# The fifth chunk of k of two attention layers, from one seven-product scheme instead of plain products in each layer

## The chip, the cores and the metric

The kernel runs on one core of one Trainium2 chip. The metric is the device time of one execution, in microseconds (us). All times here are of this one core. TensorE multiplies matrices and is called PE in the profile; VectorE is DVE, ScalarE is ACT, GpSimdE is POOL and SyncE is SP, which only issues loads and stores here. PEld is TensorE's loading of weights, which runs beside its products.

## The reference

Two cross-attention layers follow each other. Each takes the same 722 context tokens per sample (8 samples); the last 77 of them are text, the first 645 are "ip" tokens. There are 100 queries per sample, 640 channels, 20 heads of 32 channels, and context channels are 1024. Cut to what matters, one layer is:

```python
q      = x @ Wq                         # 8 x 100 x 640
k_text = text @ Wk;    v_text = text @ Wv
k_ip   = ip @ Wk_ip;   v_ip   = ip @ Wv_ip          # 8 x 645 x 640, the large products
out_text = softmax(q k_text^T * scale) v_text       # by head
sem      = q_sem . ip * scale                       # second layer only: a score per query and ip token
out_ip   = softmax(q k_ip^T * scale + 0.5 * sem) * mask @ v_ip
x = (out_text + out_ip) @ Wo + bo + x
```

The first layer has no `sem` and no mask. `k_ip` and `v_ip` depend on the context and on the layer's weights alone, not on x, so both layers' can be made at any time before they are used. Everything is float32.

## The kernel before, in words

**Units, pairs, blocks, chunks.** A unit u is a sample in a layer: u = 8 * layer + sample, 16 units in all. Two units that follow each other are a pair (8 pairs: `PAIRS`, units 0 and 1 to units 14 and 15; `LAST` is the eighth). The 645 ip tokens are five blocks (`BLOCKS`: four of 128 and one of 133). The 640 outputs of k, in rows, are five chunks of 128; chunks 0 to 3 are made together, chunk 4 is the "fifth chunk".

**Making k and v.** For each pair and block, k and v are made from the context (`x_all`, three places for a block of both samples, loaded by `load_x` in two transfers) and the weights W["k", ...] and W["v", ...]. Both use `seven` (L179): the product of a 2 by 2 block matrix of tokens (two samples by two halves of the 1024 channels) with a 2 by 2 block matrix of weights (two halves of the channels by two halves of the outputs) is made with seven products of quarters instead of eight. It costs sums: of weights, once per layer (`weight_sums`, L133 to L136), and of tokens, for each block (`token_sums`, L231: on DVE s1 at L232 and s2 at L233; s4 later by `fourth_sum`, L527 in the profile). The seven steps come in the order first, sixth, second, seventh, fifth, fourth, third. Step names mark their PSUM tile: psv_a (first and second share it), psv_b (sixth), psv_c, psv_d, psv_e. Each step's result goes from PSUM to an SBUF tile at once: first and second on ACT (L193, L202), the others on DVE (L198, L208, L213, L219, L224). The first step needs only loaded tokens; the sixth needs s2. PSUM's pool for products has two banks.

v of a block is seven steps of four matmuls (L597), with 320 columns, or 397 where the first layer's text is carried along. Chunks 0 to 3 of k are seven steps of L625: for a group of two blocks, one set for each half of the chunks; for the fifth block alone, both halves together, with 133 columns.

**The fifth chunk of k.** It has no second half of outputs to be paired with. `last_k` (L563) makes it with plain products: 8 matmuls over the 8 eighths of the channels, two samples side by side in the columns (256, or 266 in the fifth block), in two halves of four matmuls. A matmul shows as two records in the trace. The result is copied by ACT (L570) and written to `k_d` by POOL (two transfers, L572). Its weights are `W["k", 4]`, a tile loaded by `load_wk4` (one transfer of 512 KB per layer). `head` puts, ahead of the steps for v of a block, `begin` (the sums s1 and s2) and the two halves of `last_k`.

**Attention.** There are 80 steps: a unit and a chunk (four heads) each. A step makes scores against the first 512 tokens (L952, part 0), transposes of the step before (L1043, `pspt`), the scores against the other 210 (part 1), further transposes, and the products with v of the step before (`values`, L1065), copied to `hs` by DVE (L1069). The softmax of scores goes over DVE (maxima: L961 in the first layer, L967 in the second, where sem is added) and ACT (exponentials L975). Factors (DVE, L997 to L1001), scaling (ACT, four L1007; DVE L1011, L1015) follow. These pieces are put into a list, `later`, and written out one at a time: a task of production that costs time emits one piece (`next_task`); `scores` part 0 and the first transposes emit all that are left.

**Order of the work.** The order on PE, DVE and ACT is that of the program (`manual_schedule`); SP and POOL are ordered by the scheduler. k and v of pair 0 are made ahead of attention. The production of pair g + 1 is a list of tasks with costs (1.8 for a k step, 2.15 or 2.67 for v, 0 for loads and sums) that `spread` lays between the steps of the pair before, by a plan of intervals (`production`); `between` and `make` put them in. `insert` places weight loads and sums of weights at marks in the lists ("fifth j", "v j", "k j"). So layer 0's pairs 1 to 3 are made in steps 0 to 28.8, layer 1's pairs 4 to 6 in steps 28.8 to 58.8, the last pair in steps 58.8 to 78.95. The last pair is made otherwise: `last_visits` brings blocks in again, `two_chunks` (10 visits, L736 to L741) makes two chunks of k and of v at once, and `fifth_chunk` (L767) makes the fifth of k and of v by plain products (L780, L786), in 8 visits: k and v together for two blocks, then k for three, then v for three. The plan has the boundaries n + 2.9, n + 6.9 and n + 8.95, where n is step 70.

The fifth chunk is used last in a unit, as its fifth attention step (in the last pair too).

Of the kernel before, what the change touches and what calls it, by code (L numbers as in the profile page):

```python
# [28 lines left out]
NCC = CC // P  # L29
# [5 lines left out]
HK = NCC // 2  # L35
NB = 5
BLOCKS = [(j * P, (j + 1) * P if j < NB - 1 else NI) for j in range(NB)]
# [7 lines left out]
def two_layer_xattn(  # L45
# [101 lines left out]
    def load_wk(src):  # L147
        load_quarters("k", src, 2 * P)
        load_wk4(src)
# [26 lines left out]
    def product_ps(name):  # L176
        return pj[0].tile([P, 512], F32, tag="pj", name=name)
# [64 lines left out]
    with ExitStack() as es:  # L242
# [172 lines left out]
        with tc.manual_schedule(engines={mybir.EngineType.PE}):  # L415
            sums_of("k")
            text_sums()
            text_k(0)
            load_wk(wkt[1])
            text_v(0)  # L420
            sums_of("v")
            load_left(0)
            text_v_blocks(0)
            load_wv(wvt[1])
            sums_of("k")
            text_k(1)
            load_wk(wki[0])
            left_v(0)
            load_left(1)
            left_text()  # L430
            text_v(1)
            sums_of("v")
            for f in weight_sums("k", 2 * P):
                f()
            text_v_blocks(1)
            left_v(1)
# [68 lines left out]

    def quarters(at, n):
        return [x_all[:, at, i, HK * h : HK * (h + 1), :n] for i in range(2) for h in range(2)]

# [2 lines left out]
    def pair_tasks(us):  # L513
# [15 lines left out]
        for js in ((0, 1), (2, 3), (4,)):  # L529
# [15 lines left out]
            def operands(which, j, js=js, n=n, st=st, pos=pos):  # L545
# [8 lines left out]
                    return lambda k: x_all[:, at[j], i, HK * h + k, :n]  # L554
                lo, hi = sorted(at[j] for j in js)
                return lambda k: x_all[:, lo : hi + 1 : hi - lo, i, HK * h + k, :n]

            def last_k(j, half, n=n, open_={}):
                if half == 0:
                    open_[j] = product_ps(f"psk4_{us[0]}_{j}")  # L560
                ps = open_[j]
                for k in range(HK * half, HK * (half + 1)):
                    nc.tensor.matmul(  # L563
                        ps[:, : 2 * n], lhsT=W["k", 4][:, k, :], rhs=x_all[:, at[j], :, k, :n],
                        start=(k == 0), stop=(k == NCC - 1),
                    )
                if half == 0:
                    return
                o = opool.tile([P, 2, NX], F32, tag="k4", name=f"k4_{us[0]}_{j}")
                nc.scalar.copy(o[:, :, :n], ps[:, : 2 * n].rearrange("p (i n) -> p i n", i=2))  # L570
                for h, u in enumerate(us):
                    nc.gpsimd.dma_start(k_d[u][:, 4, BLOCKS[j][0] : BLOCKS[j][1]], o[:, h, :n])  # L572

            def v_steps(j, operands=operands):
                made, vo, gst = {}, {}, {}
# [188 lines left out]
        sums_ = [(0.0, lambda i=i: late[i]()) for i in range(2)]  # L764
        return begin, steps[:1] + sums_[:1] + steps[1:4] + sums_[1:] + steps[4:]

    def fifth_chunk(kinds, j, xs, at):  # L767
        n0, n1 = BLOCKS[j]
        tasks = []
        for kind in kinds:  # L770
            n = n1 - n0 if kind == "k" else P
            open_ = {}

            def half(h, kind=kind, n=n, open_=open_):
                if h == 0:
                    open_[0] = product_ps(f"ps{kind}5_{j}")
                ps = open_[0]
                if kind == "k":
                    for k in range(HK * h, HK * (h + 1)):
                        nc.tensor.matmul(  # L780
                            ps[:, : 2 * n], lhsT=W["k", 4][:, k, :], rhs=x_all[:, xs[at], :, k, :n],
                            start=(k == 0), stop=(k == NCC - 1),
                        )
                else:
                    for k in range(NCC):
                        nc.tensor.matmul(  # L786
                            ps[:, h * P : (h + 1) * P], lhsT=x_all[:, xs[at], h, k, :P],
                            rhs=wide[("wv00", "wv10")[k // HK]][:, k % HK, 2 * P : 3 * P],
                            start=(h == 0 and k == 0), stop=(k == NCC - 1), skip_group_check=True,
                        )  # L790
                if h == 0:
                    return
                t = opool.tile([P, 2, NX], F32, tag="k4", name=f"o5_{kind}_{j}")
                nc.scalar.copy(t[:, :, :n], ps[:, : 2 * n].rearrange("p (i n) -> p i n", i=2))
                for i, u in enumerate(LAST):
                    if kind == "k":
                        nc.gpsimd.dma_start(k_d[u][:, 4, n0:n1], t[:, i, :n])
                    else:
                        nc.gpsimd.dma_start(v_d[u][j * P : (j + 1) * P, 4 * P :], t[:, i, :P])

            tasks += [(1.8, lambda h=h, f=half: f(h)) for h in range(2)]
        return None, tasks


    sem_state, gs = {}, {}
# [268 lines left out]
    def production():  # L1074

        plan = []
        all_tasks = [pair_tasks(PAIRS[i]) for i in range(1, len(PAIRS) - 1)]
        parts = {}

        def sums_later(kind, n, i):  # L1080
            if kind not in parts:
                parts[kind] = weight_sums(kind, n)
            parts[kind][i]()
            if i == 3:
                del parts[kind]
# [265 lines left out]
```

## Time and profile before

| | before |
|---|---|
| median of 3 runs | 2067.76 us (2067.09 to 2068.76) |
| the profiled execution's own time | 2067.52 us |
| its span | 2065.8 us |
| granted TensorE clock, mean | 0.998 |
| DMA moved | 255.38 MB, 124 GB/s |
| stretch 0 to 225 us: TensorE, DVE, ACT busy | 219.31, 47.23, 22.29 us |
| 392 to 1050 (pairs 1 to 3 are made) | 657.33, 364.33, 267.72 of 658 |
| 1300 to 1733 (the rest of pairs 4 to 6) | 431.42, 250.82, 192.84 of 433 |
| 1733 to 1965 (the last pair, first part) | 227.18, 178.15, 132.27 of 232 |
| 1965 to 2034 (its end, steps 73 to 78) | 66.50, 53.57, 52.28 of 69 |
| 2034 to 2066 (the last step) | 24.99, 14.86, 12.51 of 32 |

The profiled execution takes 1.7 us more than its span, which runs from the first to the last instruction that the profile shows. The attention starts at about 392 us (the first maxima are at 392.2). A busy TensorE is not a stopped TensorE, but matmuls are pipelined, so a record's duration is longer than the distance to the next one's start, and prices are best read from starts in the timeline.

### The profile page before, as it was taken

To read this page: it belongs to the slowest core of one execution; us is meant where nothing else is said; L and a number is where in the kernel's file an instruction comes from. 1 tells how busy PE (TensorE), PEld (TensorE's weight loads), DVE (VectorE), ACT (ScalarE), POOL (GpSimd) and SP (SyncE) were. 2 spreads that over 40 slices of the span, in tenths; PEclk is the share of its full clock that TensorE was granted. 3 is DMA by queue.
4 is the path that set the end of the run, shared out by engine and by line. 5 is a ranking of instruction groups with operands and counts; after the bars stand their busy time and mean duration, and the time that the engine had idled before them with its cause. 6 is when DMAs were issued, how large, how long until landed. Compare 5 with 4: busy or idle time off the path is not lost.

```text
span 2065.8 us, 38497 instructions
## 1 busy us (share of the span) xinstructions
PE 2043.4 (99%) x15122; PEld 1579.3 (76%) x15122; DVE 1096.4 (53%) x2989; ACT 793.5 (38%) x2271; POOL 309.1 (15%) x445
## 2 busy tenths in 40 slices
PE   9999999999999999999999999999999999999998
PEld 8676767677778777786778777787878778888776
DVE  2211222356555655555575655556565657787775
ACT  1001000144433434334343443345444445555575
POOL 3212312111111111010110110010112011111110
PEclk9999999999999999999999999999999999999999
DMA  9545313332424443262544442262435255554471
GB/s 335 150 134 169 96 56 105 88 107 71 129 83 131 130 111 93 81 174 70 158 142 123 135 113 83 84 178 75 115 86 148 82 143 139 160 137 131 138 210 52
DMA packets 302547, 255.38 MB, mean 124 GB/s; under 512 B 46686, under 2 KB 271378, under 8 KB 302366
## 3 DMA queue, kind: packets, MB, share of 16 engines
q1 hardware_dynamic: 280590, 184.48, 32.9%
q0 software_dynamic: 21776, 68.44, 9.8%
q8 instruction: 119, 1.95, 0.4%
q14 instruction: 62, 0.51, 0.1%
HBM read 183.93 MB, written 68.93 MB: 122 GB/s over the span
## 4 chain that ended last, share of the span: by engine, by line
PE 97%; DVE 2%; ACT 1%; issue 0%; DMA 0%; SPq 0%; DVEq 0%; ACTq 0%
PE psv_a L597 8%; PE psv_d L597 8%; PE pspt L1043 8%; PE psk_a L625 6%; PE psk L563 6%; PE psk_d L625 6%; PE sc L952 6%; PE pv L1065 5%; PE psv_e L597 4%; PE psv_c L597 4%; PE psv_b L597 4%; PE psk_e L625 3%; PE psk_b L625 3%; PE psk_c L625 3%; PE pso L863 3%; PE psq L275 2%
## 5 line engine op out<-in xcount | busy, mean ns | idle before, releaser
L1050 DVE COPY pt<-pspt 128x400 f32<-128x400 f32 (+1 forms) x319 | 175.2, 569 | 147.6 <-PE pspt L1043 146.3
L975 ACT ACTIVATE p<-sc,st 100x512 f32<-100x512 f32 (+1 forms) x320 | 166.0, 531 | 198.9 <-DVE st L961 125.4
L1007 ACT ACTIVATE p<-p,st 100x512 f32<-100x512 f32 x320 | 207.5, 713 | 58.6 <-DVE st L1001 58.4
L1043 PEld LDWEIGHTS pspt<-ident,p 100*128 100x128 f32 (+1 forms) x1920 | 189.4, 138 | 46.4 <-ACT p L1007 5.6
L1043 PE MATMUL pspt<-ident,p 100*128 100x100 f32 (+1 forms) x1920 | 213.6, 251 | 8.6 <-ACT p L1007 3.0
L975 ACT ACTIVATE p<-p,st 100x512 f32<-100x512 f32 (+1 forms) x320 | 176.8, 554 | 99.0 <-DVE st L967 99.0
L597 PE MATMUL psv_a<-wv,x 128*128 128x397 f32 (+1 forms) x560 | 184.9, 472 | 0.0
L646 POOL DMA_DIRECT2D k_d<-ko x140 | 99.8, 717 | 525.5 <-DVE ko L219 477.4
L1048 ACT COPY pt<-pspt 128x400 f32<-128x400 f32 x161 | 79.3, 493 | 252.1 <-PE pspt L1043 251.9
L597 PE MATMUL psv_d<-wv,s 128*128 128x320 f32 (+1 forms) x560 | 174.9, 455 | 0.0
L597 PEld LDWEIGHTS psv_a<-wv,x 128*128 128x128 f32 x560 | 103.6, 189 | 62.1 <-issue 8.1
L967 DVE CUSTOM_DVE_ANT_0 p<-sc,sem 100x512 f32<-100x512 f32 (+1 forms) x320 | 138.8, 490 | 21.2 <-PE sc L952 20.5
L597 PEld LDWEIGHTS psv_d<-wv,s 128*128 128x128 f32 x560 | 103.4, 190 | 57.5 <-issue 5.5
L961 DVE TENSOR_REDUCE st<-sc 100x2 f32<-100x1024 f32 (+1 forms) x160 | 125.2, 824 | 30.3 <-PE sc L952 30.3
L952 PE MATMUL sc<-k,q 32*100 32x210 f32 (+1 forms) x1280 | 138.5, 502 | 0.0
L625 PE MATMUL psk_d<-s,wk 128*128 128x256 f32 (+1 forms) x672 | 136.4, 348 | 0.0
L625 PE MATMUL psk_a<-x,wk 128*128 128x256 f32 (+1 forms) x672 | 135.5, 346 | 0.0
L612 POOL DMA_DIRECT2D v_d<-vo x70 | 38.5, 550 | 634.0 <-DVE gst L587 311.1
L563 PE MATMUL psk<-x,wk 128*128 128x256 f32 (+1 forms) x560 | 132.1, 383 | 0.0
L625 PEld LDWEIGHTS psk_a<-x,wk 128*128 128x128 f32 x672 | 109.2, 189 | 20.4 <-issue 6.0
L563 PEld LDWEIGHTS psk<-x,wk 128*128 128x128 f32 x560 | 102.5, 188 | 26.1 <-issue 9.9
L625 PEld LDWEIGHTS psk_d<-s,wk 128*128 128x128 f32 x672 | 108.1, 189 | 17.8 <-issue 5.2
(209 smaller groups left out, 3252.5 us busy)
## 6 DMA issues: line engine op xcount, KB each, us to landing
x<-ip_t SPq DMA_DIRECT2D x84, 512.0 KB
k<-k_d SPq DMA_DIRECT2D x80, 322.5 KB
v<-v_d SPq DMA_DIRECT2D x80, 320.0 KB
v_d<-vo POOLq DMA_DIRECT2D x70, 320.0 KB, 2.5
k_d<-ko POOLq DMA_DIRECT2D x112, 128.0 KB, 4.8
x<-ip_t SPq DMA_DIRECT2D x22, 532.0 KB
o<-wo SPq DMA_DIRECT2D x35, 320.0 KB
q<-wq SPq DMA_DIRECT2D x20, 320.0 KB
```

Source lines behind the costliest of these rows:

```text
L563: nc.tensor.matmul(ps[:, : 2 * n], lhsT=W["k", 4][:, k, :], rhs=x_all[:, at[j], :, k, :n], start=(k == 0), stop=(k == NCC - 1),)
L597: nc.tensor.matmul(ps[:, :m], lhsT=tokens(k)[:, :P], rhs=w[:, k, :], start=(k == 0 and not go_on), stop=(k == HK - 1), skip_group_check=True,)
L625: nc.tensor.matmul(ps[:, i * m : (i + 1) * m], lhsT=W["k", WHICH[which]][:, k, r * P : (r + 1) * P], rhs=tokens(k), start=(i == 0 and k == ...
L646: nc.gpsimd.dma_start(dst[:, :, r], ko[0][:, h, :, i, p0 : p0 + n])
L952: nc.tensor.matmul(scs[i // 2][:S, i % 2, : k1 - k0], lhsT=qs_[u][rows, c, :], rhs=ks[u, c][rows, k0:k1], start=True, stop=True)
L961: nc.vector.tensor_reduce(st[:, part, 2 * h : 2 * h + 2], scs[h][:S, :, :n], AX.X, ALU.max, negate=True)
L967: nc.vector.tensor_tensor_reduce(out=p[:, i, k0 : k0 + n], in0=scs[h][:S, i % 2, :n], in1=sems[u][:, k0 : k0 + n], scale=-1.0, scalar=3.0e ...
L975: nc.scalar.activation(dst, dst if l else scs[h][:S, i % 2, :n], AF.Exp, bias=st[:, part, i : i + 1], scale=-1.0 if l else 1.0, accum_out= ...
L1007: nc.scalar.activation(p[:, i, :KA], p[:, i, :KA], AF.Copy, scale=mul[:, 0, i : i + 1])
L1043: nc.tensor.transpose(ps[:rows, i * S : (i + 1) * S], pr[u, c][:, i, j * P : j * P + rows], ident[:S, :S])
L1050: nc.vector.tensor_copy(dst, src)
L1065: nc.tensor.matmul(ps[32 * i : 32 * i + 32, :S], lhsT=lhs, rhs=pt[:rows, j, i * S : (i + 1) * S], start=(j == 0), stop=(j == 5),)
```

## The change

The fifth chunks of both layers are paired with each other. The token matrix is as before; the weight matrix has the two halves of the channels by the two layers. One scheme of seven products, `k4_steps`, thus makes the fifth chunk of k for both layers, in the pairs of the first layer, and writes it to `k_d` of units u and u + 8. For a group of two blocks a step is four matmuls with 256 columns, and 133 for the fifth block alone (four transfers to `k_d` per block). It uses the sums s1, s2 and s4 that `begin` made for the group. The pairs of the second layer make no fifth chunk of k.

The weights of this scheme, b11 to b22 and the sums t2 to t4 (t1 is written over b12), are 256 KB tiles (`W4`): two in the place of the old `wk4` tile, two in the two buffers "sem", and three in "g", "kt5" and "gt", tiles that the second layer's semantic scores use. `load_w4` issues four transfers; `w4_sums` makes four sums on DVE.

What else moves: `head` is now `begin` alone, so v's steps follow it at once. In pair 0, `load_w4` comes behind the second begin, `w4_sums` and `k4_steps` follow k's second set. In the later pairs of the first layer, `k4_steps` comes between v and k of the group. The loads of `wk4` are gone, the marks "fifth j" are replaced by places within v ("v 0", "v 1"). In the last pair, `fifth_chunk` makes v alone, so there are 5 visits instead of 8. The boundaries of the plan are n + 3.4 and n + 8.95, instead of n + 2.9, n + 6.9 and n + 8.95. A result tile takes its place among the buffers "made", not in "k4".

```diff
-            load_wk(wki[0])
+            load_quarters("k", wki[0], 2 * P)
...
+    def load_w4():
+        pair = wpool.tile([P, 2, HK, P], F32, tag="wk4", name="w4_a")
+        at = [pair[:, i] for i in range(2)]
+        for pool, tag in ((tpool, "sem"), (tpool, "sem"), (one, "g"), (one, "kt5"), (one, "gt")):
+            t = pool.tile([P, HK * P], F32, tag=tag, name=f"w4_{len(at)}")
+            at.append(t.rearrange("p (k n) -> p k n", k=HK))
+        for x, t in zip(("b11", "b12", "b21", "b22", "t2", "t3", "t4"), at):
+            W4[x] = t
+            if x[0] == "b":
+                i, l = int(x[1]) - 1, int(x[2]) - 1
+                nc.sync.dma_start(
+                    t, wki[l].rearrange("(k p) n -> p k n", p=P)[:, HK * i : HK * (i + 1), 4 * P :]
+                )
+        W4["t1"] = W4["b12"]
+
+    def w4_sums():
+        nc.vector.tensor_tensor(W4["t3"], W4["b22"], W4["b12"], ALU.subtract)
+        nc.vector.tensor_tensor(W4["t2"], W4["t3"], W4["b11"], ALU.add)
+        nc.vector.tensor_tensor(W4["b12"], W4["b12"], W4["b11"], ALU.subtract)
+        nc.vector.tensor_tensor(W4["t4"], W4["b21"], W4["t2"], ALU.subtract)
...
-            def last_k(j, half, n=n, open_={}):
...
+            def k4_steps(js=js, n=n, operands=operands, pos=pos):
+
+                made, ko = {}, {}
+                m = n * len(js)
+
+                def product(ps, which, go_on):
+                    tokens = operands(which, None if len(js) == 2 else js[0])
+                    for k in range(HK):
+                        nc.tensor.matmul(
+                            ps[:, :m], lhsT=W4[WHICH[which]][:, k, :], rhs=tokens(k),
+                            start=(k == 0 and not go_on), stop=(k == HK - 1), skip_group_check=True,
+                        )
...
+                return [(1.75 if len(js) == 2 else 0.95, lambda i=i: step(i)) for i in range(7)]
 
-            def head(j, begin=begin, last_k=last_k):
+            def head(j, begin=begin):
 
-                return [(0.0, lambda: begin(j))] + [(1.8, lambda i=i: last_k(j, i)) for i in range(2)]
+                return [(0.0, lambda: begin(j))]
...
-                tasks += head(0) + [v_load] + head(1) + with_sums(0, with_sums(1, ks_[:7])) + [v_sums] + ks_[7:]
+                tasks += head(0) + head(1) + [(0.0, load_w4), v_load] + with_sums(0, with_sums(1, ks_[:7]))
+                tasks += [v_sums] + ks_[7:] + [(0.0, w4_sums)] + k4_steps()
                 tasks += v[:2] + [(0.0, text_sum)] + v[2:] + v_steps(1)
             else:
                 for j in js:
-                    tasks += head(j)
-                    marks[f"fifth {j}"] = len(tasks)
-                    tasks += with_sums(j, v_steps(j))
+                    tasks += head(j) + with_sums(j, v_steps(j))
...
-                tasks += ks_
+                tasks += ([] if l else k4_steps()) + ks_
...
-    def fifth_chunk(kinds, j, xs, at):
+    def fifth_chunk(j, xs, at):
...
-            ("fifth 4", 0, [(0.0, lambda: load_wk4(wki[1]))]),
...
-            ("fifth 0", 1, v[2:3]), ("fifth 0", 0, v[3:]),
-            ("fifth 1", 1, k[:1]), ("fifth 1", 0, k[1:2]), ("v 1", 6, k[2:3]), ("v 1", 4, k[3:]),
+            ("v 0", 7, v[2:3]), ("v 0", 6, v[3:]),
+            ("v 1", 7, k[:1]), ("v 1", 6, k[1:2]), ("v 1", 5, k[2:3]), ("v 1", 3, k[3:]),
...
-        for kinds, js in (("kv", every[:2]), ("k", every[2:]), ("v", every[2:])):
-            visits += [(j, lambda j, xs, i, kinds=kinds: fifth_chunk(kinds, j, xs, i)) for j in js]
+        visits += [(j, fifth_chunk) for j in every]
...
-            (n - 10 - AHEAD, n + 2.9, lists[: 2 * NB]),
-            (n + 2.9, n + 6.9, lists[2 * NB : 3 * NB]),
-            (n + 6.9, n + 8.95, lists[3 * NB :]),
+            (n - 10 - AHEAD, n + 3.4, lists[: 2 * NB]),
+            (n + 3.4, n + 8.95, lists[2 * NB :]),
```

More of the change, by code (lines that the diff above doesn't have):

```diff
@@ L504, in load_res @@
         resg[g] = t
+    W4 = {}
+    def load_w4():
[17 more added lines that the diff above has]
+        nc.vector.tensor_tensor(W4["t4"], W4["b21"], W4["t2"], ALU.subtract)
     def quarters(at, n):
@@ L556, in operands @@
                 return lambda k: x_all[:, lo : hi + 1 : hi - lo, i, HK * h + k, :n]
-            def last_k(j, half, n=n, open_={}):
[L559 to L572, printed above, removed]
             def v_steps(j, operands=operands):
@@ L648, in k_steps, with step @@
                 return [(1.8, lambda i=i: step(i)) for i in range(7)]
-            def head(j, begin=begin, last_k=last_k):
-                return [(0.0, lambda: begin(j))] + [(1.8, lambda i=i: last_k(j, i)) for i in range(2)]
+            def k4_steps(js=js, n=n, operands=operands, pos=pos):
[8 more added lines that the diff above has]
+                        )
+                def step(i):
+                    if i == 0:
+                        o = ko[0] = opool.tile([P, 2, 2, m], F32, tag="made", name=f"k4_{us[0]}_{js[0]}")
+                        made[0] = seven(
+                            f"psk4_{us[0]}_{js[0]}", product, tuple(o[:, h, l2] for h in range(2) for l2 in range(2))
+                        )
+                    made[0][i]()
+                    if i < 6:
+                        return
+                    for h, u in enumerate(us):
+                        for l2 in range(2):
+                            for j in js:
+                                nc.gpsimd.dma_start(
+                                    k_d[u + B * l2][:, 4, BLOCKS[j][0] : BLOCKS[j][1]],
+                                    ko[0][:, h, l2, pos[j] * n : (pos[j] + 1) * n],
+                                )
+                return [(1.75 if len(js) == 2 else 0.95, lambda i=i: step(i)) for i in range(7)]
+            def head(j, begin=begin):
+                return [(0.0, lambda: begin(j))]
             def with_sums(j, steps, fourth_sum=fourth_sum):
@@ L765, in two_chunks @@
         return begin, steps[:1] + sums_[:1] + steps[1:4] + sums_[1:] + steps[4:]
-    def fifth_chunk(kinds, j, xs, at):
[L768 to L802, printed above, removed]
@@ new lines, in fifth_chunk, with half @@
+    def fifth_chunk(j, xs, at):
+        open_ = {}
+        def half(h):
+            if h == 0:
+                open_[0] = product_ps(f"psv5_{j}")
+            ps = open_[0]
+            for k in range(NCC):
+                nc.tensor.matmul(
+                    ps[:, h * P : (h + 1) * P], lhsT=x_all[:, xs[at], h, k, :P],
+                    rhs=wide[("wv00", "wv10")[k // HK]][:, k % HK, 2 * P : 3 * P],
+                    start=(h == 0 and k == 0), stop=(k == NCC - 1), skip_group_check=True,
+                )
+            if h == 0:
+                return
+            t = opool.tile([P, 2, P], F32, tag="made", name=f"o5_{j}")
+            nc.scalar.copy(t, ps[:, : 2 * P].rearrange("p (i n) -> p i n", i=2))
+            for i, u in enumerate(LAST):
+                nc.gpsimd.dma_start(v_d[u][j * P : (j + 1) * P, 4 * P :], t[:, i])
+        return None, [(1.8, lambda h=h: half(h)) for h in range(2)]
```

## The prediction

> **What bounds the kernel now.** I read the page first: busy times, the slices, the chain that ended last.
>
> ```profile
> span 2065.8 us, 38497 instructions
> ...
> PE 2043.4 (99%) x15122; PEld 1579.3 (76%) x15122; DVE 1096.4 (53%) x2989; ACT 793.5 (38%) x2271; POOL 309.1 (15%) x445
> ...
> DVE  2211222356555655555575655556565657787775
> ...
> PE 97%; DVE 2%; ACT 1%; issue 0%; DMA 0%; SPq 0%; DVEq 0%; ACTq 0%
> ```
>
> TensorE is the bound, with only 22 us of the span idle, at a granted clock of 0.998. So any product removed shortens the kernel, if nothing else becomes late in its place. The DVE digits tell where that can happen: 5 to 6 tenths through the pairs, 7 to 8 in the last sixth. The busy time alone would therefore mislead; what counts is what DVE delivers to TensorE, and when. The view of groups by form gives the products that the change replaces (count, then total us and mean ns):
>
> ```profile
> L563 PE MATMUL psk<-x,wk 128*128 128x256 f32 x448 | 104.6, 381 | 0.0
> L625 PE MATMUL psk_a<-x,wk 128*128 128x133 f32 x224 | 28.4, 278 | 0.0
> L563 PE MATMUL psk<-x,wk 128*128 128x266 f32 x112 | 27.4, 391 | 0.0
> L780 PE MATMUL psk<-x,wk 128*128 128x256 f32 x64 | 15.6, 386 | 0.0
> L780 PE MATMUL psk<-x,wk 128*128 128x266 f32 x16 | 4.0, 389 | 0.0
> ```
>
> Matmuls overlap, so a price is the distance between starts, not the mean duration. In the timeline the 8 records of psk_a begin at 212.93 and those of psk_b at 214.66: 1.73 us for 8 records of 256 columns, 0.216 each. The 16 records of 266 columns at 336.86 last until 340.45: 3.59, 0.224 each. The 16 of 133 columns at 357.60 last until 359.43: 1.83, 0.114 each.
>
> **TensorE's own work.** Removed, per pair: four blocks of 16 records (4 x 3.46) and the fifth (3.59), 17.43 us; eight pairs, 139.4. Added, per pair of the first layer: two groups of 7 products of 8 records (2 x 7 x 1.73 = 24.2) and 7 products of 8 records with 133 columns (7 x 0.915 = 6.4), 30.6 us; four pairs, 122.4. **Net -17.0 us**, the eighth product: +13.2 in each pair of the first layer, -17.4 in each of the second.
>
> The 133-column row is the one to doubt. Its group shows 0.53 of the time for 0.52 of the columns of the 256-column group, so it is priced by columns. [...]
>
> **Begin's cover.** Before, a block went: begin (DVE sums s1 L232, s2 L233), the fifth chunk (3.46 us on TensorE), then v's psv_a, then psv_b, which needs s2. The head is now begin alone. DVE executes in order: s1 stands behind the eviction L224 of the previous product, and behind whatever attention work was written ahead of it. The timeline at 1594 to 1610, DVE first, then TensorE:
>
> ```profile
> 1597.74 0.42 DVE L224 TENSOR_TENSOR ko<-psk_d,ko 128x256 f32<-128x256 f32 x1 [1.30 <-PE psk_d L625]
> 1598.94 0.26 DVE L1069 COPY hs<-pv 128x100 f32<-128x100 f32 x1 [0.78 <-PE pv L1065]
> 1599.95 0.69 DVE L967 CUSTOM_DVE_ANT_0 p<-sc,sem 100x512 f32<-100x512 f32 x1 [0.75 <-PE sc L952]
> ...
> 1602.40 0.69 DVE L232 TENSOR_TENSOR s<-x 128x512 f32<-128x512 f32 x1
> 1603.12 0.69 DVE L233 TENSOR_TENSOR s<-s,x 128x512 f32<-128x512 f32 x1
> ```
> ```profile
> 1597.63 1.06 PE L1065 MATMUL pv<-pt,v 128*32 128x100 f32 x40
> ...
> 1598.80 1.12 PE L952 MATMUL sc<-k,q 32*100 32x512 f32 x8
> 1599.85 3.73 PE L563 MATMUL psk<-x,wk 128*128 128x256 f32 x16
> ...
> 1603.73 2.32 PE L597 MATMUL psv_a<-wv,x 128*128 128x320 f32 x8
> 1605.89 0.85 PE L1043 MATMUL pspt<-ident,p 100*128 100x100 f32 x8
> 1606.58 2.34 PE L597 MATMUL psv_b<-wvt,s 128*128 128x320 f32 x8
> ```
>
> Count from the end of the previous product (1597.7). s2 ends 6.1 later, since four L967 reductions (2.45 us) stand ahead of it; psv_b starts 8.9 later, so 2.8 of slack. Without the psk line (3.56) that slack is -0.8, even with these transposes (0.69) in between. At other places of the changed order nothing lies between: pv 1.17, scores 1.04, psv_a 2.0, so psv_b is ready at +4.2 to +4.3 and s2 at +6.1. Where nothing of attention stands between, s2 comes at 0.49 + 0.68 + 0.69 = +1.9 and psv_a covers it (2.0, or 2.5 in layer 0 with the text columns): no cost.
>
> By the changed order of both engines, block by block, the late ones:
> - four L967 ahead of the sums, five blocks (third and fourth of units 10 and 12, fifth of 10): 1.8, 1.6, 1.8, 1.6, 2.0, together 8.8
> - the first block of unit 8, behind the 1.37 us weight sum L134/L135 and the last eviction of pair 6: s2 at 5.0 to 5.6 (5.59 in the block at 1047.8) against 2.7: 2.7
> - third block of unit 8, behind two L961 reductions (1.2 us each): 1.0
> - second blocks of units 4 and 6, behind the six reductions after the second scores: 0.7 each, 1.4
>
> Sum **13.9 us**. Bounds: 1 if DVE runs ahead wherever I have it behind; 16 if each block's lag is as long as in the worst row (6.1). I take 13.9, nearest to the four measured lags (6.11, 5.93, 5.59, 3.57).
>
> **k of the fifth block.** Its new products last 0.92 us, half of any seven-product step before, and two PSUM banks alternate, so each eviction has about a step to be done. DVE is held up to 2.4 us by the factors (L997 to L1001, L1015), ACT 2.56 by four L1007. Where the changed order puts these among them, in pairs 2, 4 and 6, I get 1.6, 1.8, 1.8: **5.2 us**, bounds 1 (k's other narrow row, psk_b, shows no wait) and 7. The 256-column groups have the shape and evictions of the existing k steps, which show no wait: 0, bounds 0 and 2. In pair 0 the four weight sums (0.69 each, 2.8) are covered by seven products (12 us) but for 0.3 before the second product.
>
> **Tail, steps 73 to 78** (1965.0 to 2034.3, 69.3 us). The last pair loses 17.4 us of products, 13.9 of it here, 3.5 in 58 to 72. But the steps have a second chain: pv, copy to hs, factors, four L1007, first transposes. It already shows in the step at 2010.24:
>
> ```profile
> 2012.73 0.23 DVE L1001 SCALAR_TENSOR_TENSOR st<-st,mask_sb 100x8 f32<-100x8 f32 x1
> ```
> ```profile
> 2013.06 2.56 ACT L1007 ACTIVATE p<-p,st 100x512 f32<-100x512 f32 x4 [2.35 <-DVE st L1001]
> ```
> ```profile
> 2015.67 0.65 PE L1043 MATMUL pspt<-ident,p 100*128 100x100 f32 x5 [0.31 <-ACT p L1007]
> ```
>
> From the scores (2011.41) to the last head is 4.3 us whatever TensorE has to do; scores 1.05 and one task 1.9 fill 3. Steps 76, 77 and 78, with 9.3, 11.1 and 9.6 us of products, idle 0.23, 0.61 and 1.67. With 13.9 us spread out of all six steps, and factors now emitted behind the values in 73 to 75 too, I take 1.2 each in five steps, 6.2. And the write of step 74's k moves a step later: last product about 2.9 us into step 73, write landing 5.5, load 3.0, ready at some +13 against 10.7 of work: 2. Together **8.2** of the 13.9 lost; bounds 5 (0.6 as in step 77 more in each, and 2 for k) and 11.
>
> **Steps 58 to 72**: DVE at 66 to 89%, less TensorE work to hide behind: **0.7**, bounds 0 and 3.
>
> **At nothing**: the second layer's load of 512 KB and six loads of x fall away on SP, which is no bound (in the waits, TensorE waits for one load only, 4.2 us for the first weights). POOL issues the same 80 k_d writes, more of them early, where POOL is 1 to 3 tenths busy. The new weights (four DMAs) are waited for only if their tiles come free after 229 us; the first stage's pool ends by about 210, and a 512 KB load takes some 4 us: covered by 12 us of ks products; without that cover 1 to 4. Their places are taken again by scores of step 38 on, and the last k4 product runs by step 29.
>
> **Sum**: -17.0 + 13.9 + 5.2 + 0.3 + 8.2 + 0.7 = +11.3. On the profiled execution's own time 2067.52 that is 2078.8; the median of the runs, 2067.76, stands 0.24 above. Forecast **2079**, by itself 2072 to 2084: begin 4.9 (to 9), k 3.2 and tail 3.2 less, or 2.1, 1.8, 2.8 and 2.3 more, taken as independent (root of the squares 6.7 and 4.5).
>
> **Rivals.**
> 1. *Faster: DVE is ahead.* If s1 and s2 are done before psv_a ends, TensorE stays the bound up to step 72. Place: ten begins and three narrow k groups. Price: -17.0 + 1 + 1 + 8.2 + 0.7 + 0.3 = -5.8: 2061.7. It decides where s2 lies under +4.2 (+2.0 where nothing else is between). For it: DVE 53% busy, no waits for sums in the pairs before. Against: those were covered by 3.46 us, and 2.8 was the slack.
> 2. *No change: half covered.* Begin's stalls at 6, for DVE makes up part during the preceding stall, narrow k 2: -17 + 6 + 2 + 8.2 + 1 = +0.2: 2067.7.
> 3. *Full gain*: the tail's chain also shrinks, all covered: 2067.5 - 17 + 1 = 2051.5. The waits of steps 77 and 78 speak against it.
> 4. *Worse*: all upper ends, -17 + 16 + 7 + 11 + 3 + 2 + 0.3 = +22: 2090, with every block at its longest lag.
>
> That the change does not do what it says is excluded by its order: 128x256 and 128x133 products in seven groups, no psk line of sixteen.
>
> **Chances.** Forecast 0.56, rival 1 0.16, rival 2 0.18, rival 3 0.05, rival 4 0.05. A measurement here separates about 0.2% (4.1 us): faster is under 2063.6, slower over 2071.9. Faster: rivals 1 and 3, 0.21. Within: rival 2, and 0.02 of the forecast's low edge, 0.20. Slower 0.59. Range 2061 to 2086, which leaves out rivals 3 and 4 and the edges.
>
> **What would show it.** PE's busy time 2026; in the waits, psv_b behind L233 near 14 us (rival 1: under 2); psk4 tiles behind evictions near 5; pspt behind ACT's p 8 to 10, not 3.0; steps 73 to 78 64 us, not 55. If the new narrow records lie over 0.12 us apart, or the weights are awaited before step 0, the prediction is wrong elsewhere.

## The result, and the profile after

The changed kernel takes 2088.33 us (median of four runs, 2087.69 to 2089.18) against 2068.26 for the kernel before in the same measurement: ratio 1.0098, 95% interval 1.0081 to 1.0116. It is slower by 20.1 us, where 11.3 were forecast; the time lies 2.3 us over the top of the range. The profiled execution takes 2089.18, its span is 21.6 us longer than before.

The page, the same lines as before and the row of the granted clock (PEclk):

```profile
span 2087.4 us, 38776 instructions
...
PE 2041.9 (98%) x15154; PEld 1578.1 (76%) x15154; DVE 1119.4 (54%) x3053; ACT 785.1 (38%) x2255; POOL 309.1 (15%) x445
...
DVE  2211222355555555555557566656565657777775
...
PEclk9999999999999999999999999999999999999998
...
PE 92%; DVE 5%; ACT 1%; issue 1%; DMA 0%; SPq 0%; DVEq 0%; ACTq 0%
```

TensorE's busy time fell by only 1.5 us, not by 17.0. That could be read as products that weren't saved. It is not so: where a step has no wait in either kernel, its length changed by what its products changed, to 0.05 us. Busy time rose again: of the 15.5 us, some 9.5 are in steps 73 to 78, where the same products took longer (the clock's row shows an 8 at the end), and some 6 lie before step 58, most of it beside waits, as shown below. In the chain that ended last, DVE's share went from 2% to 5%, some 60 us more of the chain.

The waits of TensorE (engine, tile, line, releaser: total us, times, longest). The lines have moved: v's products L597 are L605 now, scores L952 L976, the maxima L967 L991, the scaling L1007 L1031, transposes L1043 L1067, the products with v L1065 L1089; the new products of `k4_steps` are L666, and L1074 (DVE) and L1072 (ACT) copy transposes to pt:

```profile
PE psv_b L605 <- DVE s L233: 11.4, 8, 2.9
PE pspt L1067 <- ACT p L1031: 5.5, 14, 1.3
...
PE pspt L1067 <- DVE pt L1074: 3.4, 5, 0.8
...
PE pv L1089 <- DVE pt L1074: 2.0, 3, 0.7
...
PE psk_d L666 <- DVE k L213: 1.3, 2, 0.6
PE psk_c L666 <- DVE k L198: 1.1, 3, 0.4
...
PE sc L976 <- DMA k<-k_d: 0.9, 1, 0.9
```

The first line is begin's lost cover, a row of 11.4 us that the list of before doesn't have. The two of L666 are the narrow products' evictions. One place from the timeline, TensorE then DVE:

```profile
1418.21 1.12 PE L976 MATMUL sc<-k,q 32*100 32x512 f32 x8
1419.25 2.42 PE L605 MATMUL psv_a<-wv,x 128*128 128x320 f32 x8
1421.51 0.49 PE L860 MATMUL psm<-ident,gt 128*77 128x128 f32 x3
1423.28 2.42 PE L605 MATMUL psv_b<-wvt,s 128*128 128x320 f32 x8 [1.27 <-DVE s L233]
```
```profile
1421.20 0.69 DVE L991 CUSTOM_DVE_ANT_0 p<-sc,sem 100x512 f32<-100x512 f32 x1
...
1421.81 0.69 DVE L232 TENSOR_TENSOR s<-x 128x512 f32<-128x512 f32 x1
1422.53 0.69 DVE L233 TENSOR_TENSOR s<-s,x 128x512 f32<-128x512 f32 x1
```

No psk line stands between the scores and psv_a any more. s2 ends at 1423.22, psv_b starts 0.06 later; the sums stood behind the last of four reductions. The step that holds this wait is 1.54 us longer than its products account for, though only 1.27 are shown as idle: a matmul's record ends later than the next one can start (psv_a's last ends at 1421.67, psm starts at 1421.51), so this wait cost 0.27 us more than its entry. By the same reckoning the eight waits of psv_b, 11.4 us by their entries, lengthened their steps by 13.4, some 0.25 more for each.

**Where the 21.6 us are.** Steps are counted from the first scores of a step to those of the next.

| stretch | before | after | change | of it products | lost |
|---|---|---|---|---|---|
| up to step 58 | 1710.0 | 1732.1 | +22.1 | +0.5 | 21.6 |
| steps 58 to 72 | 255.0 | 250.7 | -4.3 | -3.5 | -0.8 |
| steps 73 to 78 | 69.3 | 73.7 | +4.4 | -13.9 | 18.3 |
| step 79 | 31.43 | 30.87 | -0.6 | 0 | -0.6 |

Lost is the change in length beyond that of the products.

The view of windows over the six steps 73 to 78 gives the surprise. Its columns are the stretch and its length; busy time of TensorE, weight loads, DVE, ACT, POOL, each with its instructions; then the granted clock, the DMA share and GB/s. Before, steps 73, 77 and 78:

```profile
1965.00:1977.30 12.30, 12.30 (x140) 10.20 (x137) 9.30 (x34) 9.14 (x27) 2.18 (x4) 1.00 0.90 257
...
2011.40:2023.10 11.70, 11.09 (x140) 9.23 (x136) 9.12 (x34) 8.79 (x26) 1.22 (x3) 1.00 0.39 106
2023.10:2034.30 11.20, 9.53 (x124) 7.39 (x120) 9.12 (x34) 8.53 (x25) 1.99 (x4) 1.00 0.10 33
```

After, steps 74, 75, 76 and 78:

```profile
1995.10:2005.90 10.80, 9.38 (x120) 7.41 (x120) 8.44 (x31) 8.64 (x25) 0.92 (x2) 1.00 0.79 216
2005.90:2019.30 13.40, 11.36 (x125) 9.11 (x120) 9.21 (x34) 8.85 (x25) 1.21 (x3) 0.87 0.32 92
2019.30:2033.00 13.70, 10.92 (x108) 8.12 (x104) 9.24 (x34) 8.48 (x24) 0.00 (x0) 0.75 0.19 53
...
2044.90:2056.50 11.60, 10.23 (x108) 7.45 (x104) 9.15 (x34) 8.53 (x25) 1.07 (x2) 0.76 0.13 41
```

Steps 75 to 78 are longer than before though the six have 13.9 us of products less, and in three of the six the granted clock is 0.87, 0.75 and 0.76. In the timeline 16 records of one kind take 2.05 us early in step 75 and 3.60 later in it:

```profile
2006.97 2.05 PE L814 MATMUL psv<-wv,x 128*128 128x128 f32 x16
...
2011.59 1.05 PE L1067 MATMUL pspt<-ident,p 100*128 100x100 f32 x8 [0.76 <-DVE pt L1074]
...
2013.11 3.60 PE L814 MATMUL psv<-wv,x 128*128 128x128 f32 x16
```

TensorE's waits in these six steps:

```profile
PE pspt L1067 <- ACT p L1031: 4.1, 10, 1.3
PE pspt L1067 <- DVE pt L1074: 3.4, 5, 0.8
PE pv L1089 <- DVE pt L1074: 2.0, 3, 0.7
PE pv L1089 <- ACT pt L1072: 1.0, 2, 0.8
PE sc L976 <- DMA k<-k_d: 0.9, 1, 0.9
```

Of the 18.3 us lost there, 8.8 are more idle time (11.3 instead of 2.5). By the lists, only some 2.9 of them are waits for the scaled softmax weights (L1031, 4.1 against 1.2 before) and 0.9 for k; some 5.2 are waits for the copies to pt (L1074 and L1072, 6.4 against 1.2). The lower clock is an estimate: it was 0.50 for 15.9 us of these steps (0.87 or 0.75 is the mean of a step), 0.3 of them idle, and half of the rest is 7.8. The other 1.7 no row names; a little more than its entry for each of some fourteen more waits would be that much, which is not shown.

### The profile page after: what moved, and what is told of

Read it like the earlier page. It is cut to its first block, busy times and chain, and to the rows that moved or that the text cites. A ratio compares the mean times of both kernels' runs of the same rounds, so it can differ in the third digit from the quotient of the medians.

```text
span 2087.4 us, 38776 instructions
## 1 busy us (share of the span) xinstructions
PE 2041.9 (98%) x15154; PEld 1578.1 (76%) x15154; DVE 1119.4 (54%) x3053; ACT 785.1 (38%) x2255; POOL 309.1 (15%) x445
## 4 chain that ended last, share of the span: by engine, by line
PE 92%; DVE 5%; ACT 1%; issue 1%; DMA 0%; SPq 0%; DVEq 0%; ACTq 0%
PE psv_d L605 8%; PE pspt L1067 8%; PE psv_a L605 7%; PE psk_a L633 6%; PE psk_d L633 6%; PE sc L976 6%; PE pv L1089 5%; PE psv_e L605 4%; PE psv_b L605 4%; PE psv_c L605 4%; PE psk_c L633 3%; PE psk_b L633 3%; PE psk_e L633 3%; PE pso L887 3%; PE psk_d L666 2%; PE psq L275 2%
## 5 line engine op out<-in xcount | busy, mean ns | idle before, releaser
L1031 ACT ACTIVATE p<-p,st 100x512 f32<-100x512 f32 x320 | 207.6, 713 | 66.0 <-DVE st L1025 65.8
L1067 PE MATMUL pspt<-ident,p 100*128 100x100 f32 (+1 forms) x1920 | 217.6, 254 | 13.9 <-ACT p L1031 5.5
L1067 PEld LDWEIGHTS pspt<-ident,p 100*128 100x128 f32 (+1 forms) x1920 | 191.4, 139 | 52.0 <-ACT p L1031 8.6
L1074 DVE COPY pt<-pspt 128x400 f32<-128x400 f32 (+1 forms) x319 | 174.9, 568 | 103.5 <-PE pspt L1067 96.1
L1072 ACT COPY pt<-pspt 128x400 f32<-128x400 f32 x161 | 79.1, 491 | 284.4 <-PE pspt L1067 284.0
L605 PE MATMUL psv_a<-wv,x 128*128 128x397 f32 (+1 forms) x560 | 185.5, 473 | 0.0
L605 PE MATMUL psv_d<-wv,s 128*128 128x320 f32 (+1 forms) x560 | 174.3, 454 | 0.0
L605 PEld LDWEIGHTS psv_a<-wv,x 128*128 128x128 f32 x560 | 103.1, 190 | 67.6 <-issue 12.6
L991 DVE CUSTOM_DVE_ANT_0 p<-sc,sem 100x512 f32<-100x512 f32 (+1 forms) x320 | 138.7, 490 | 20.0 <-PE sc L976 18.9
L605 PEld LDWEIGHTS psv_d<-wv,s 128*128 128x128 f32 x560 | 104.2, 190 | 54.7 <-issue 4.3
L976 PE MATMUL sc<-k,q 32*100 32x210 f32 (+1 forms) x1280 | 140.0, 507 | 0.9 <-DMA k<-k_d 0.9
L605 PE MATMUL psv_b<-wvt,s 128*128 128x320 f32 x280 | 83.0, 439 | 11.5 <-DVE s L233 11.4
L605 PE MATMUL psv_e<-wvt,x 128*128 128x397 f32 (+1 forms) x280 | 92.6, 473 | 0.0
```

Source lines behind the costliest of these rows:

```text
L605: nc.tensor.matmul(ps[:, :m], lhsT=tokens(k)[:, :P], rhs=w[:, k, :], start=(k == 0 and not go_on), stop=(k == HK - 1), skip_group_check=True,)
L976: nc.tensor.matmul(scs[i // 2][:S, i % 2, : k1 - k0], lhsT=qs_[u][rows, c, :], rhs=ks[u, c][rows, k0:k1], start=True, stop=True)
L991: nc.vector.tensor_tensor_reduce(out=p[:, i, k0 : k0 + n], in0=scs[h][:S, i % 2, :n], in1=sems[u][:, k0 : k0 + n], scale=-1.0, scalar=3.0e ...
L1031: nc.scalar.activation(p[:, i, :KA], p[:, i, :KA], AF.Copy, scale=mul[:, 0, i : i + 1])
L1067: nc.tensor.transpose(ps[:rows, i * S : (i + 1) * S], pr[u, c][:, i, j * P : j * P + rows], ident[:S, :S])
L1072: nc.scalar.copy(dst, src)
```

## The experiments

Theory: the losses are (1) the sums behind attention work, (2) the narrow evictions, (3) in the tail the chain through the factors, and (4) a clock that falls since TensorE waits often there. Rivals: that DVE is merely shifted, that a narrow step is too short by itself, and, for the tail, that the clock or the late transfers have another reason.

| run | what | median us | ratio to before, 95% interval |
|---|---|---|---|
| | the changed kernel | 2088.33 | 1.0098, 1.0081 to 1.0116 |
| e1 | changed, sums directly behind the product before | 2078.02 | 1.0051, 1.0035 to 1.0068 |
| e2 | changed, no softmax pieces among narrow products | 2086.18 | 1.0089, 1.0074 to 1.0104 |
| e3 | changed, pieces early in steps 73 to 79 | 2078.28 | 1.0047, 1.0032 to 1.0062 |
| e4 | changed, products of no use in the tail | 2089.88 | 1.0105, 1.0090 to 1.0120 |
| e5 | before, last pair as changed, k's fifth chunk left out | 2066.78 | 0.9995, 0.9986 to 1.0005 |
| e6 | e5 with pieces early | 2055.39 | 0.9942, 0.9925 to 0.9959 |
| e7 | before with pieces early | 2062.20 | 0.9973, 0.9963 to 0.9983 |
| e8 | changed with e1, e2, e3, two weight sums earlier | 2064.56 | 0.9983, 0.9973 to 0.9992 |
| e9 | e8, the weight sums earlier still | 2060.18 | 0.9966, 0.9954 to 0.9979 |

### e1: the sums directly behind the product before

In `production`, each `begin` is merged with the last costed task ahead of it, together with the loads between:

```diff
-                return [(0.0, lambda: begin(j))]
+                return [(-1.0, lambda: begin(j))]
...
+                if t < 0 and before:
+                    where, k = before
+                    t0, f0 = where[k]
+                    fs = [f0] + [f_ for _, (_, f_) in held] + [f]
...
+                    where[k] = (t0, lambda fs=fs: [g_() for g_ in fs])
```

> The changed kernel, with the sums s1 and s2 of each block written directly behind the last step of the product before, ahead of the attention work that stood between; TensorE's order is unchanged. Theory (the missing cover of begin costs time, 11.4 us of waits of psv_b for s2 in eight places): these waits fall to about 2, what is left at the first block of unit 8, where a weight sum still stands ahead, and the time falls by 10 to 13 us, to about 2076. Rival (DVE only moves the lateness to the maxima of the scores, which then come 1.4 us later): the waits of psv_b go, the time falls by less than 4.

Measured: 2078.02, 10.3 us less than the changed kernel. What is left of the row in the list of TensorE's waits:

```profile
PE psv_b L605 <- DVE s L233: 2.4, 1, 2.4
```

Seven of eight waits are gone, and the maxima, which now stand behind the two sums (1.4 us) on DVE, made no new one: in steps 29 to 57 idle time is 1.5 us instead of 9.5, and the stretch 605.7 instead of 615.4. The theory holds. The profiled execution is 14.4 us shorter than the changed kernel's: 11.6 up to step 58, and 2.8 behind it, where the edit changes nothing and the clock was low for a shorter time (by the means of steps 73 to 79, at 0.50 for some 14 us instead of 26).

### e2: no softmax pieces among the narrow products

```diff
-                return [(1.75 if len(js) == 2 else 0.95, lambda i=i: step(i)) for i in range(7)]
+                return [(1.75 if len(js) == 2 else 0.0 if i else 6.65, lambda i=i: step(i)) for i in range(7)]
```

> The changed kernel, with the cost of the fifth block's seven new products put on the first of them, so that no pieces of softmax are written out between them. Theory (their evictions come late behind such pieces; 3.3 us of waits, and by steps some 4 to 5 lost in pairs 2, 4 and 6): the waits of psk4 go and the time falls by 3 to 5 us. Rival (a 0.92 us step is too short for its eviction by itself): the waits stay, under 1 us gained.

Measured: 2086.18, 2.2 us less; the intervals of the two ratios overlap, so the median does not settle it. In the trace, psk_d's waits went, psk_c's rose from 1.1 to 1.7, and steps 0 to 28 took 706.9 us instead of 708.8. Behind step 58 this trace is 2.7 us shorter too, with no less idle time, at a higher clock (by the means of steps 73 to 79, 0.50 for some 14 us instead of 26), which the edit does not touch. So both are likely true in part: the pieces cost about 2, and a narrow step (0.9 us) is also short by itself for an eviction that stands behind any DVE work.

### e3: pieces early in steps 73 to 79

```diff
             if last:
+                if n >= NC_ * LAST[0] + 3:
+                    emit(len(later))
                 values(*last)
```

> The changed kernel, with all pending pieces of softmax written out ahead of the values in steps 73 to 79, so that the factors stand ahead of the copy to hs on DVE. Theory (steps 73 to 78 lose 8.8 us more to waits of the chain through the factors, and some 9 to a granted clock of 0.76 to 0.87 that comes of these waits): the factors start 2 to 3 us earlier, waits in 73 to 78 fall from 11 to 4 to 6, the clock there stays at 0.95 or more, and the time falls by 10 to 15 us. Rival (the clock falls there for another reason, such as the end of the transfers): 3 to 6 us gained, the clock stays under 0.9.

Measured: 2078.28, 10.1 less. Steps 73 to 78 take 65.3 instead of 73.7 and step 79 27.51 instead of 30.87. TensorE's waits for L1031 fell from 4.1 to 0.6 there. The clock is 1.00 in five of the six steps, in step 76 it still fell:

```profile
2006.00:2016.30 10.30, 9.20 (x124) 7.38 (x120) 9.11 (x35) 8.64 (x25) 1.04 (x3) 1.00 0.38 107
2016.30:2029.00 12.70, 10.85 (x111) 8.25 (x104) 8.79 (x33) 8.48 (x24) 0.16 (x1) 0.73 0.24 67
```

So the expected gain came, but not all that was expected of the waits (8.4 idle, not 4 to 6) and the clock. Most of the gain is not idle time: of the 8.4 us in steps 73 to 78 idle time gives 2.9 and busy time 5.5 (the clock was at 0.50 for 6.8 us instead of 15.9), and the 3.4 in step 79 are busy time alone, at a mean clock of 0.97 instead of 0.83, with 6.4 idle instead of 6.0. The waits for pt stayed (6.9 instead of 6.4). What the edit moves can be seen in the changed kernel's step 76: the text exponentials were done at 2016.2 (ACT, L1018), but the factors that need them came after the copy of the values:

```profile
2019.45 0.26 DVE L1093 COPY hs<-pv 128x100 f32<-128x100 f32 x1 [1.36 <-PE pv L1089]
2019.63 0.46 DVE L1021 TENSOR_REDUCE st<-p 100x4 f32<-100x308 f32 x1
```

### e4: products of no use in the tail

In `transposes` and ahead of `values`, in steps 73 to 78:

```diff
+        if j == 0 and in_tail[0]:
+            for _ in range(6):
+                nc.tensor.matmul(ps[:, 400:512], lhsT=ident, rhs=ident[:, :112], start=True, stop=True)
...
+                    for _ in range(4):
+                        nc.tensor.matmul(spare[0][:, 1, 384:496], lhsT=ident, rhs=ident[:, :112], start=True, stop=True)
```

> The changed kernel, with ten products more per step in steps 73 to 78, of 112 columns, whose results are not read: six ahead of the first transposes, four ahead of the values; some 2 us per step, 12 in all, of which some 8 fall into waits. Theory (the clock falls since TensorE waits often): the clock stays at 1.00 in 73 to 78 and the time falls by 4 to 8 us although work is added. Rival (waits alone make the loss, the clock is not governed by them): the time rises by 2 to 6 us, the clock stays under 0.9.

Measured: 2089.88, no gain; the clock is 1.00 in all six steps. Two of them:

```profile
2009.00:2020.90 11.90, 11.34 (x146) 9.61 (x142) 9.21 (x34) 8.64 (x25) 1.07 (x2) 1.00 0.33 96
2020.90:2032.80 11.90, 10.22 (x128) 8.00 (x124) 9.20 (x34) 8.36 (x24) 0.00 (x0) 1.00 0.25 71
```

Each theory is half right. That the clock fell because TensorE had too little to do is shown, by one trace of six steps: transfers, other engines and the order are the same, only work was added, and the clock came back from 0.87, 0.75 and 0.76 in three of the steps to 1.00; steps 75 and 76, 13.4 and 13.7 us, take 11.9 although they do more. But the filling, some 12 us, was not hidden as far as I reckoned (5.2 us of idle time left, from 11.3), steps 73 and 74 grew by 1.7, and step 79, unfilled, was 1.4 slower at a clock of 0.81. Step 73 also began 1.4 us later in this trace (1984.2 instead of 1982.8), ahead of the filling. e3, whose edit starts at step 73 too, lost as much in step 28: 30.5 us at a clock of 0.94, where the changed kernel takes 29.0 at 1.00 with the same 2.9 us wait of psv_b. The time expected, 4 to 8 less, is a miss.

### e5, e6, e7: the tail alone

e5 is the kernel before with the changed kernel's `fifth_chunk`, its visits and boundaries. The fifth chunk of k of the last pair is not computed; two_chunks fills its place with copies of another chunk:

```diff
+                if r:
+                    nc.gpsimd.dma_start(k_d[u][:, 4, n0:n1], o[0][:, h, 0, P : P + n])
...
-        for kinds, js in (("kv", every[:2]), ("k", every[2:]), ("v", every[2:])):
+            visits += [(j, fifth_chunk) for j in every]
```

> The kernel before, with the last pair alone as in the change: its fifth chunk of k isn't computed (its place in k_d is filled with copies of another chunk), five visits for v, boundaries n + 3.4 and n + 8.95. That takes 17.4 us of products off TensorE in the last pair, and adds none elsewhere. Theory (the factors' chain and the lower clock in steps 73 to 78 eat what is removed there, 13.9 us): the time stays within 3 us of before, waits in 73 to 78 near 11 us, the clock under 0.9 in at least two of these steps. Rival (the products are worth their time, and the changed kernel's tail is slow for another reason, such as its moved transfers): 12 to 17 us faster than before.

Measured: 2066.78, ratio 0.9995 with an interval that holds 1. **17.4 us of products less, with nothing added, are worth nothing that can be measured.** Steps 73 to 78 take 76.2 us instead of 69.3, with 11.8 us idle; the clock is under 0.9 in five of the six. Two of them:

```profile
1983.90:1997.30 13.40, 11.36 (x129) 8.83 (x123) 9.24 (x34) 8.82 (x25) 1.22 (x3) 0.87 0.33 94
1997.30:2010.70 13.40, 10.74 (x112) 7.87 (x108) 9.23 (x34) 8.48 (x24) 0.00 (x0) 0.75 0.20 52
```

This run has no seven-product fifth chunk, no missing cover and none of the moved weights. The tail's loss is its own. The boundaries and visits moved along with the products, and no run separates the two.

e6 adds the edit of e3 to it.

> The run before this one (the last pair alone as in the change, its fifth chunk of k left out), and all pending pieces of softmax written out ahead of the values in steps 73 to 79. Theory (the chain is what eats the gain): 8 to 12 us faster than without the early pieces, so 2056 to 2061. Rival: under 4 us faster.

Measured: 2055.39, 11.4 less than e5 and 12.7 under before in the same measurement: most of the products' worth is there as soon as the chain is shorter. Steps 73 to 78 take 64.2. Again less of it is waits than clock: of the 12.0 us, 3.2 are idle time, and the clock was at 0.50 for 3.4 us instead of 20.3.

e7 is the kernel before with the edit of e3 alone.

> The kernel before, with the early pieces in steps 73 to 79 alone. Theory (before, only steps 76 to 79 wait for the chain, 2.3 us in 77 and 78 and part of 6.8 in 79): 2 to 5 us faster. If the early pieces were good for more than the chain's waits, more than 6.

Measured: 2062.20, 5.8 us less than before: in the traces 2.0 in steps 73 to 78, 3.8 in step 79 (27.67). A little more than expected. Step 79 before, then in e7:

```profile
2034.30:2065.60 31.30, 24.71 (x265) 20.62 (x260) 14.86 (x48) 12.42 (x31) 0.00 (x0) 0.85 0.11 36
```
```profile
2033.40:2061.00 27.60, 21.07 (x264) 18.22 (x260) 14.69 (x48) 12.42 (x31) 0.00 (x0) 0.95 0.13 41
```

Idle time in the whole step is 6.75 and 6.61 us, nearly the same; what fell is the busy time of the same products, by 3.6, at a higher clock. So the late pieces cost time before too, with all its products as cover, but in the last step they cost it through the clock, not through longer waits.

### e8, e9: the edits together

> The changed kernel with the three edits together (sums directly behind the product before; the narrow products' cost on the first; pieces early in steps 73 to 79), and the second of the weight sums for the second layer's v put one step earlier, out of the way of the first block of unit 8. Theory (the losses are separate: 10 to 13, 2 to 3, 10 and 2): 2061 to 2066, some 4 us faster than before. Rival (they overlap, since one wait hides the next): over 2068.

Measured: 2064.56, 23.8 less than the changed kernel and 3.5 under before in the same measurement. The sums of the edits (10.3, 2.2 and 10.1) make 22.6, so they are separate. The edit puts both weight sums one step earlier, not the second alone, and that gave nothing: psv_b still waited 2.4 us at the first block of unit 8, as in e1, and was itself slow behind that wait, 3.41 us instead of the 2.34 of as many records of psv_a:

```profile
1105.16 2.34 PE L605 MATMUL psv_a<-wv,x 128*128 128x320 f32 x8
1109.89 3.41 PE L605 MATMUL psv_b<-wvt,s 128*128 128x320 f32 x8 [2.39 <-DVE s L233]
```
```profile
1102.95 1.49 DVE L134 TENSOR_TENSOR wvt<-wv,wv 128x1280 f32<-128x1280 f32 x1
...
1104.70 1.48 DVE L135 TENSOR_TENSOR wvt<-wvt,wv 128x1280 f32<-128x1280 f32 x1
```

Both weight sums, 3.0 us, stand between the last evictions of the pair of units 6 and 7. (The prediction and the expectations call a pair by its first unit: their pairs 2, 4 and 6 are pairs 1, 2 and 3 of layer 0.) e9 puts them two steps earlier than e8, which is three steps earlier than the changed kernel; against the latter:

```diff
-            ("k 4", 1, v[:1]),
-            ("k 4", 0, v[1:2] + [(0.0, lambda: load_quarters("k", wki[1], 2 * P))]),
+            ("k 4", 4, v[:1]),
+            ("k 4", 3, v[1:2]),
+            ("k 4", 0, [(0.0, lambda: load_quarters("k", wki[1], 2 * P))]),
```

> The run e8 with the first two weight sums for the second layer's v (DVE, 1.49 us each) three steps earlier still, at the third and fourth of the last seven products of pair 6. Theory (the 2.4 us that psv_b still waits at the first block of unit 8 are these two sums, which stand ahead of its own sums on DVE; TensorE's clock halves right behind that wait, 1.1 us more): the wait falls under 0.5 and the time by 2.5 to 4 us against e8, to 2060.5 to 2062. Rival (the weights themselves arrive late, so the sums only wait for their load): no gain.

Measured: 2060.18, 4.4 less than e8. The two were measured apart: against before in its own measurement e8 is 3.5 less and e9 6.6, so some 3 is the edit's. The trace agrees: the wait went from 2.4 to 0.6, and step 28 takes 29.5 us instead of 32.9, with 1.2 us idle instead of 3.0. e9 is faster than both kernels, by 28 us and, at a ratio of 0.9966, by 0.34%. But e7, which leaves the change out and has one edit of two lines, is at 0.9973 and the intervals overlap: with all its losses repaired as far as tried, the change is worth nothing measurable over that.

## Why the prediction was wrong

- **Products, -17.0**: right. The narrow records cost what their columns cost: in the slowest tile (psk_d) 32 of them make 4.6 us of records at 286 ns, against 15.4 at 382 for 64 wide ones, the two means of before (278 and 381) but for their waits, and their starts lie 0.114 us apart, against 0.216 for the wide ones.
- **Begin's cover, 13.9**: right in mechanism, and in eight of nine places. The eight waits show 11.4 and cost 13.4; e1 gave back 10.3 with one wait left. Rival 1 (DVE is ahead) fell here.
- **k of the fifth block, 5.2**: a little too high. Six waits show 2.8 us; the five steps that hold them (7, 17, 18, 27, 28) are 4.3 longer than their products and psv_b's waits account for. The places were right. e2 gave back about 2; a rest stays without pieces.
- The two and 0.3 make 19.4 up to step 58; 21.6 were lost. That they lie near is in part luck: the two terms were 1.4 too high together, and two losses were not in the sum. About 2.2 us are lost ahead of step 0, where I had 0.3. The first weights came 0.45 us later (4.65 instead of 4.20) and k's first products began 1.1 later, in a part that is the same in both; e5, e6 and e7, whose start is that of before, wait 4.6, 4.8 and 4.9 us for the first weights. Then two of pair 0's k products waited, 1.1 by their starts (0.6 idle for an eviction on ACT, L193, which before had the fifth chunk ahead of it, and 0.2). Some 1.7 us are spread over other steps.
- **Steps 58 to 72, 0.7**: -0.8.
- **Tail, 8.2, bounds 5 and 11: this is the step that failed.** It measured 18.3. The idle time rose by 8.8, which is near 8.2 by luck. Of the 6.2 for the factors' chain 2.9 came (L1031), of the 2 for k of step 74 0.9 (the three terms that I gave for k, 2.9, 5.5 and 3.0, make 11.4 and not 13, so 0.7 over the 10.7 of work); 5.2 came in waits for the copies pt, which the chain as I wrote it does not have. And the sum took TensorE's price per product from rows at full clock for a stretch in which it would idle some sixth of the time. The clock cost some 7.8, and 1.7 more are in no row. The measured time less these 9.5 is about 2079, since the other misses nearly cancel. A row of before already spoke of it, the last step's:

```profile
2034.00:2066.00 32.00, 24.99 (x268) 20.78 (x268) 14.86 (x48) 12.51 (x32) 0.00 (x0) 0.85 0.11 36
```

In step 79, with 6.75 us idle of 31.4, the clock is 0.85. I read that clock and left it out of the sum.

The range failed with that step: its top end took the waits at their highest, and no term for the clock. Two of the signs that the prediction named showed it: TensorE's busy time was 2041.9, not 2026, and steps 73 to 78 took 73.7 us, not 64. A third missed the other way: pspt waited 5.5 us for ACT's p, not 8 to 10.

## What to carry to other kernels

A product that is removed pays only where TensorE is the last to arrive (in e5, 17.4 us of products less gave a ratio of 0.9995): price the second chain of that stretch first, and look whether a neighbour in the order was the cover for a sum or an eviction. A small task between two others may be the only thing that hides an in-order engine's lateness (here 3.46 us of products, and 11.4 us of waits in eight places without them); when it goes, move what it hid ahead of the work that stands before it. Where TensorE is going to wait often, its price per product is not that of the busy stretches (here 2.05 and 3.60 us for the same 16 records in one step).

## What the runs showed of the hardware

TensorE's granted clock fell in the changed kernel's steps 75, 76 and 78 though no wait in them is longer than 1.3 us. In steps 75 and 76, 2.0 and 2.8 us of idle time in pieces of 0.2 to 1.3 us went with 0.87 and 0.75; in before's step 78, 1.7 us of 11.2 went with 1.00. With 2.0 us idle, step 75 had 1.00 in e1 and 0.87 in the changed kernel. In e1 four runs of one kernel took 2074.78, 2076.98, 2079.06 and 2079.57 us at mean clocks of 0.997, 0.994, 0.994 and 0.992: the fastest run has the highest clock, the slowest the lowest.

The means by step hide when the clock was low. In the changed kernel's tail it was at 0.50 from 2013.3 to 2016.8 us, from 2023.6 to 2030.4 and from 2050.9 to 2057.7, and at 1.00 in the two stretches between. The stretch ahead of the last of these falls, and the one behind it:

```profile
2047.50:2050.90 3.40, 2.03 (x17) 1.44 (x15) 3.40 (x11) 3.40 (x9) 0.00 (x0) 1.00 0.00 0
2050.90:2054.30 3.40, 3.40 (x23) 2.32 (x21) 1.96 (x12) 2.13 (x7) 1.07 (x2) 0.50 0.13 49
```

TensorE was idle for 1.4 us of the first. As much idle time did not always go with a fall: from 1108.8 to 1112.2 us, in the longest wait of psv_b, it was idle for 1.8 of 3.4 us, and the clock was at 1.00 there and in the 3.4 us behind. So a count of the idle time does not tell by itself where the clock falls. In e4, where only work was added, it was at 1.00 in all six steps; what else decides it is not shown.
